# A four-layer graph transformer on one core: other chunk sizes at the end of a layer, the last V in one piece, V earlier in layer 3

## The chip, the cores and the metric

The kernel runs on one NeuronCore of a Trainium2 chip. The metric is the device time of one execution in microseconds; the number for the kernel before is the median of three runs. A profile is one further execution, recorded by the hardware profiler.

## The reference, cut to what matters

There are 3327 nodes with 256 features and a random adjacency matrix with about 0.5 per cent of ones, some 16 neighbours a node. Layer 0 is a small graph attention. Layers 1 to 3 are transformer layers in which a node attends to its neighbours only:

```python
qkv = layer_norm(x, g1, be1) @ w_qkv                 # 256 -> 768
q, k, v = ...                                        # 8 heads of 32
scores = jnp.einsum('nhd,mhd->hnm', q, k) * SCALE
scores = jnp.where(mask, scores, -jnp.inf)           # mask = adj != 0
attn = jax.nn.softmax(scores, axis=-1)
out = jnp.einsum('hnm,mhd->nhd', attn, v).reshape(n, DIM)
x = x + out @ w_proj + b_proj
h2 = layer_norm(x, g2, be2)
ff = jax.nn.gelu(h2 @ w1 + b1) @ w2 + b2             # 256 -> 1024 -> 256
return x + ff
```

Layer L+1 needs k and v of all nodes: a neighbour can lie anywhere.

## The kernel before, in words

**Phase 0** (lines 623 to 1208) reads the adjacency matrix, computes layer 0 and q, k, v of layer 1, lists every node's neighbours and sorts the nodes by their number of neighbours. After that there are 26 blocks of 128 nodes. Block b has `CAPS[b]` neighbour slots for each node, 40 for block 0 down to 10 for block 25.

**Layers 1 to 3** (class `Layer`, from line 1277) work on a table `kv[L]` in device memory, one row with k and v per node. `issue` (line 1288) fetches one *group*: up to four neighbour slots of one block, one indirect DMA (line 1303, on the GpSimd queue, POOL) for each slot, 128 rows of 2 KB each. The groups land in a ring of `NBUF` = 10 tiles. The blocks are taken in the order 25, 1, 24, 2, ..., 14, 12, 13, 0 (`ORDER`), so that block 0 with its ten groups comes last.

**A turn** of the loop in `run` (line 1568) handles one group:

- `scores` multiplies k by q (line 1325) and sums by head (line 1326), both on VectorE (DVE);
- after a block's last group `softmax` takes the minimum of the negated scores (line 1337, DVE) and the exponential (line 1340, ScalarE, ACT), and `take_q` copies the next block's q (line 1311, ACT);
- `value` does V for an earlier group: `weights` once for a block (lines 1346 to 1353, DVE), then `values`: v times weight (line 1366, DVE), then transposes that add the slots up in PSUM (line 1372, TensorE, PE). After that the tile of the ring is free, and `values` calls `issue` for the next group. V for a block begins in the second turn after its exponential. In the turns of block 0 two groups of V are done per turn;
- `some` (line 1544) hands out the rest of the work. There are two lists. `short` holds a finished block's copy (line 1390), projection (lines 1394 to 1396) and residual add with the statistics of the norm (line 1400). `long` holds the steps of a *chunk* of blocks, each with a cost.

**Chunks.** When the last block of a chunk has had its add, `chunk` (line 1411) puts these steps into `long`: the norm's scale (13 small DVE operations), the normalised blocks and their transposes (lines 588 and 591), up, Gelu and down in 8 pieces (lines 1439, 1445, 1462; line 1455 for a chunk of one block), shift and transposes back (lines 1468 and 1476), one add a block (line 1480), and in layers 1 and 2 the next layer's norm, q, k, v (`qkv`, line 1492) and `keep`, which copies k and v out of PSUM (line 1498), scales q (line 1499) and stores the row block to `kv[L + 1]` (line 1500). In layer 3 `store` writes the output instead (line 1505). The next layer's first gather waits until all rows are stored.

**The rate.** `self.rate` is credit per turn: the cost of all steps in `long`, divided by a number of turns (lines 1404 to 1407). It is set when a chunk's steps are added. Every call of `some` adds the rate to the credit, at most 8, and takes steps as long as the credit is above 0. Chunks before the change have 3, 4, 4, 4, 4, 4, 2 and 1 blocks. The divisor is the number of groups in the next four blocks less 2, and 5 for the chunk ahead of block 0. After the turns come the values that are left (block 0's ten groups), each followed by `some`; then `some` alone at rate 4.

The program order on each engine is the order in which these functions are called. Nothing is reordered later; an engine waits where its next instruction has to wait.

Of the kernel before, what the change touches and what calls it, by code (L numbers as in the profile page):

```python
# [8 lines left out]
FP = mybir.dt.float32  # L9
BF = mybir.dt.bfloat16  # L10
I32 = mybir.dt.int32
AF = mybir.ActivationFunctionType
# [5 lines left out]
P = 128  # L18
N = 3327
D = 256  # L20
HEADS = 8
# [11 lines left out]
NB = (N + P - 1) // P  # L33
# [27 lines left out]
CB = 4  # L61
# [447 lines left out]
@with_exitstack  # L509
def kernel(ctx: ExitStack, tc: tile.TileContext, ins, out: bass.AP):  # L510
    nc = tc.nc
    keep = ctx.enter_context(tc.tile_pool(name="s_keep", bufs=1))
    dram = ctx.enter_context(tc.tile_pool(name="s_dram", bufs=1, space=DRAM))
    flag = keep.tile([1, 1], I32, name="flag")
    E = mybir.EngineType
    with tc.manual_schedule(engines={E.PE, E.DVE, E.Activation, E.Pool, E.SP}):
        with ExitStack() as inner:
            sparse_path(inner, tc, ins, out, dram, flag)
    unfit = nc.values_load(flag[0:1, 0:1])
    with tc.If(unfit > 0):  # L520
        general_path(tc, ins, out)


def sparse_path(ctx, tc, ins, out, dram, flag):
    nc = tc.nc
    const = ctx.enter_context(tc.tile_pool(name="s_const", bufs=1))
    small = ctx.enter_context(tc.tile_pool(name="s_small", bufs=4))

    ident = const.tile([P, P], FP, name="s_ident")
# [12 lines left out]
    kv = {1: dram.tile([PADDED + 1, KVW[1]], FP, name="kv1"),  # L542
          2: dram.tile([PADDED, KVW[2]], FP, name="kv2"),
          3: dram.tile([PADDED, KVW[3]], FP, name="kv3")}
# [78 lines left out]
    with tc.tile_pool(name="a", bufs=1) as a, tc.tile_pool(name="aw", bufs=2) as aw, \  # L623
# [462 lines left out]
        for g in reversed(range(NG)):  # L1086
            at = dict(zip(names, (0, 1, 3, 4, 5, 6, 7, 8, 9, 10, 11, 12)))
# [179 lines left out]

    ORDER = [b for k in range(NB // 2) for b in (NB - 1 - k, k + 1)][:NB - 1] + [0]
    CHUNK, at = {}, 0
    for n in [CB - 1] + [CB] * ((NB - CB - 2) // CB) + [2, 1]:  # L1270
        for b in ORDER[at:at + n]:
            CHUNK[b] = ORDER[at:at + n]
        at += n
    assert at == NB
    slots = {b: [(b, s) for s in range(0, CAPS[b], GS)] for b in ORDER}

    class Layer:
# [102 lines left out]
        def block(self, b):  # L1380
            L, w, c = self.L, self.w, {}
            x = t2[:, b, :D]
            chunk = CHUNK[b]
            if b == chunk[0]:
                self.n2 = Norm(len(chunk), f"f{L}_{b}")
            n2 = self.n2

            def copy_T():
                c["oT"] = work.tile([P, 2 * P], FP, tag="oT", name=f"oT_{L}_{b}")
                nc.scalar.copy(c["oT"], self.po[b][:, :2 * P])  # L1390

            def project():
                ps = self.po[b][:, D:]
                nc.tensor.matmul(ps, ones_bf[:96, :], bias3[:, 0, :], start=True, stop=False)  # L1394
                for k in range(2):
                    nc.tensor.matmul(ps, c["oT"][:, k * P:(k + 1) * P], w["w_proj"][:, k, :],  # L1396
                                     start=False, stop=(k == 1))

            def add():
                nc.vector.tensor_add(x, x, self.po.pop(b)[:, D:])  # L1400
                n2.stats(chunk.index(b), x)
                if b == chunk[-1]:
                    self.long += self.chunk(chunk, n2)
                    at = ORDER.index(b) + 1
                    turns = sum(len(slots[i]) for i in ORDER[at:at + CB])
                    turns = 5 if at == NB - 1 else turns - 2
                    self.rate = sum(cost for cost, _ in self.long) / max(turns, 1)

            return [lambda: None, copy_T, project, lambda: None, add]

        def chunk(self, blocks, n2):
            L, w, nxt = self.L, self.w, self.nxt
            n = len(blocks) * P
# [81 lines left out]
            def keep(j):  # L1495
                b = blocks[j]
                kvr = work.tile([P, 2 * D], FP, tag="kvr", name=f"kvr_{L}_{b}")
                nc.scalar.copy(kvr, c["pk", j])
                nc.scalar.mul(t2[:, b, D:2 * D], c["pq", j][:, :D], -HD ** -0.5)
                nc.scalar.dma_start(kv[L + 1][b * P:(b + 1) * P, :], kvr)  # L1500

            def store(j):
                b = blocks[j]
# [27 lines left out]
            if nxt is not None:  # L1531
                steps += [at(2, lambda: c["n1"].scale()), *(at(2, t) for t in turns("n1", "n")),
                          at(2, lambda: to_hT("n1", "n", nxt["g1"], nxt["be1"])),
                          at(3, lambda: qkv(0))]
                for j in js:
                    fs = [lambda j=j: keep(j)]
                    if j + 1 < len(blocks):
                        fs.append(lambda j=j: qkv(j + 1))
                    steps.append(at(3, *fs))
            else:  # L1540
                steps += [at(1, lambda j=j: store(j)) for j in js]
# [12 lines left out]
                self.short.pop(0)()  # L1554

        def run(self):
            for _ in range(NBUF):
                self.issue()
            self.take_q(ORDER[0])

            todo, wait = [], {}

            def value():
                if todo[0][1] == 0:
                    self.weights(todo[0][0])
                self.values(*todo.pop(0))

            for k, b in enumerate(ORDER):
                for g in slots[b]:
                    self.scores(*g)  # L1570
                    if g == slots[b][-1]:
                        self.softmax(b)
                        if k + 1 < NB:
                            self.take_q(ORDER[k + 1])
                    for i in wait:
                        wait[i] += 1
                    for _ in range(2 if len(todo) > NBUF // 2 or b == 0 else 1):
                        if todo and wait[todo[0][0]] > 1:
                            value()
                    self.some()  # L1580
                todo += slots[b]
                wait[b] = 0
            while todo:
                value()
                self.some()
            self.rate = 4.0
            while self.short or self.long:
                self.some()
# [45 lines left out]
```

## Time and profile before

| what | us |
|---|---|
| median of three runs | 2573.75 (2568.12 to 2575.34) |
| the profiled execution | 3158.07 |
| its span, first to last instruction | 3156.3 |
| POOL: first gather of layer 2 | 1428.53 |
| POOL: last gather of layer 1 begins | 1310.82 |
| busy: DVE, PE, POOL, ACT | 1935.3, 1794.0, 1362.7, 774.6 |
| gathers of k and v rows (line 1303) | 1344, of 947 ns each |
| scores: multiply, sum (lines 1325, 1326) | 363 each, of 1138 and 1141 ns |
| V multiply (line 1366) | 363, of 1128 and 1221 ns |
| mean granted PE clock | 0.735 |

The profiled execution took 584 us longer than the median of the runs. So shares of the span are not shares of the metric, and a stage's length is taken over only where the text says why. "Busy" counts the time an instruction executes. The forty slices of the page are 78.9 us each, a digit is a tenth of busy time. "A <- B: total, times, longest" in the list of waits means that the engine and line A stood still until B ended; "remote" is a wait whose releaser the profile can't name, "issue" time without a wait that it shows.

### The profile page before, as it was taken

Reading aid. Unit: us, or ns where it says so; the run is one execution under the profiler, and the core shown is the slowest. Engines: PE = TensorE matmul, PEld = TensorE weight load, DVE = VectorE, ACT = ScalarE, POOL = GpSimd, SP = SyncE. Lnnn points to the kernel's source line nnn. Section 1 sums busy time; section 2 is a strip of 40 time slices with the busy share of each in tenths; the row PEclk is TensorE's granted clock in tenths of the full one; section 3 lists DMA queues with packets and bytes.
Section 4 is the critical chain, followed back from the end, with each engine's and each line's share of the span. In section 5 each row is a group of like instructions: output and inputs, shape, how many; then the busy total and the mean of one; then the engine's idle time right before and its main releaser. Section 6 shows DMA issues by size and latency. Waiting matters only on the chain.

```text
span 3156.3 us, 24036 instructions
## 1 busy us (share of the span) xinstructions
PE 1794.0 (57%) x7561; PEld 1163.5 (37%) x7561; DVE 1935.3 (61%) x3983; ACT 774.6 (25%) x1316; POOL 1362.7 (43%) x1458
## 2 busy tenths in 40 slices
PE   4767752255666666671457667666713435665556
PEld 3645531133333333350334333433512323433334
DVE  6688995457657656533656756755446556656554
ACT  4455621012222222230112212222300111212112
POOL 4000004545555554305555555544054555565550
PEclk9868766577787886785578778878755766776768
DMA  5334306645555565415455555555064554554560
GB/s 207 131 117 148 129 31 204 174 138 169 165 172 162 156 174 152 112 51 177 141 156 156 163 160 150 175 152 140 24 189 125 156 155 135 169 163 147 161 156 13
DMA packets 144486, 453.80 MB, mean 144 GB/s; under 512 B 29521, under 2 KB 40156, under 8 KB 141021
## 3 DMA queue, kind: packets, MB, share of 16 engines
q0 software_dynamic: 113056, 370.26, 40.9%
q1 hardware_dynamic: 9834, 53.90, 4.9%
q10 hardware_dynamic: 21458, 28.02, 2.5%
q8 instruction: 61, 1.00, 0.1%
q14 instruction: 77, 0.63, 0.1%
HBM read 420.64 MB, written 31.42 MB: 143 GB/s over the span
## 4 chain that ended last, share of the span: by engine, by line
DVE 25%; issue 18%; PE 18%; another core or an unknown queue 17%; POOL 11%; ACT 5%; DMA 5%; DVEq 0%; ACTq 0%; POOLq 0%; SPq 0%
POOL kv L1303 11%; DVE kv L1325 5%; DMA kv<-kv,t 4%; DVE sc L1326 3%; DVE vw L1366 3%; PE pu L1439 3%; PE po L1372 3%; PE py L1462 2%; DVE cand L735 2%; PE pk L1492 1%; PE s_pk L1010 1%; ACT s_aT L724 1%; DVE s_v L731 1%; PE pf L591 1%
## 5 line engine op out<-in xcount | busy, mean ns | idle before, releaser
L1303 POOL DMA_INDIRECT kv<-kv,t x1344 | 1273.0, 947 | 1210.3 <-issue 534.2
L1372 PE MATMUL po<-s_ident,vw 128*128 128x128 f32 x2688 | 475.4, 334 | 580.2 <-DVE vw L1366 387.2
L1372 PEld LDWEIGHTS po<-s_ident,vw 128*128 128x128 f32 x2688 | 395.5, 174 | 724.1 <-issue 373.5
L1325 DVE TENSOR_TENSOR kv<-kv,q 128x1024 f32<-128x1024 f32 (+3 forms) x363 | 413.1, 1138 | 397.1 <-ACT q L1311 274.6
L1366 DVE TENSOR_TENSOR vw<-kv,w 128x1024 f32<-128x1024 f32 x333 | 371.4, 1128 | 87.2 <-remote 84.6
L1326 DVE TENSOR_REDUCE sc<-kv 128x32 f32<-128x1024 f32 (+3 forms) x363 | 414.1, 1141 | 12.4
L1439 PE MATMUL pu<-fT,s_w 128*128 128x512 f32 (+3 forms) x768 | 341.2, 579 | 62.3 <-issue 35.8
L1462 PE MATMUL py<-gT,s_w 128*128 128x512 f32 (+2 forms) x672 | 321.8, 597 | 58.1 <-issue 50.2
L1400 DVE TENSOR_TENSOR t<-t,po 128x256 f32<-128x256 f32 x78 | 32.6, 418 | 390.8 <-remote 254.5
L1445 ACT ACTIVATE gT<-pu,pvb 128x512 f32<-128x512 f32 (+3 forms) x192 | 115.7, 607 | 628.2 <-remote 384.1
L1439 PEld LDWEIGHTS pu<-fT,s_w 128*128 128x128 f32 x768 | 157.4, 222 | 196.1 <-issue 146.4
L1462 PEld LDWEIGHTS py<-gT,s_w 128*128 128x128 f32 x672 | 132.6, 206 | 180.7 <-issue 144.0
L1396 PEld LDWEIGHTS po<-s_w_proj,oT 128*128 128x128 f32 x312 | 71.8, 255 | 281.8 <-issue 272.3
L1394 PE MATMUL po<-bias,s_ones_bf 96*128 96x256 bf16 x78 | 25.2, 324 | 259.7 <-issue 147.4
L1390 ACT COPY oT<-po 128x256 f32<-128x256 f32 x78 | 28.9, 371 | 548.5 <-remote 320.2
L711 POOL MEMSET s_abf<- 128x1 bf16 x23 | 2.2, 104 | 361.4 <-DVE s_v L731 253.7
L1492 PE MATMUL pk<-s_w_qkv,nT 128*128 128x512 f32 x208 | 128.4, 748 | 22.0 <-ACT nT L596 9.9
L735 DVE MAX8 cand<-s_v 128x8 f32<-128x208 bf16 x416 | 118.0, 360 | 0.9
L1396 PE MATMUL po<-s_w_proj,oT 128*128 128x256 f32 x312 | 113.1, 500 | 0.0
L723 PE MATMUL s_ptb<-s_ident_bf,s_abf 128*128 128x128 bf16 x676 | 67.1, 265 | 68.3 <-ACT s_abf L714 45.2
L591 PE MATMUL pf<-s_ident,xn_f 128*128 128x128 f32 x156 | 46.1, 444 | 86.8 <-ACT xn_f L588 66.7
L855 PE MATMUL s_pa<-s_aT,s_hs 128*128 128x256 bf16 x338 | 82.3, 290 | 13.2 <-DVE s_hs L817 13.2
(288 smaller groups left out, 2252.1 us busy)
## 6 DMA issues: line engine op xcount, KB each, us to landing
s_a<-in_adj_dram SPq DMA_DIRECT2D x25, 1663.5 KB
kv<-kv,t POOLq DMA_INDIRECT x1344
kv<-kvr ACTq DMA_DIRECT2D x52, 256.0 KB
kv<-s_kvr ACTq DMA_DIRECT2D x26, 256.0 KB
s_w<-in_L_gnn_w_dram SPq DMA_DIRECT2D x6, 1024.0 KB
t<-ql ACTq DMA_DIRECT2D x6, 592.0 KB
t<-s_x ACTq DMA_DIRECT2D x6, 512.0 KB
s_w_qkv<-in_L_gnn_w_qkv_dram SPq DMA_DIRECT2D x3, 768.0 KB
```

Source lines behind the costliest of these rows:

```text
L735: nc.vector.max(out=self.cand[:, s, :], in_=self.v[:, s, :])
L855: nc.tensor.matmul(self.pa[:, c0:c0 + 2 * P], S.hs[:r, k, :P], aT[:r, k, :], start=(k == 0), stop=(k == NB - 1))
L1303: nc.gpsimd.indirect_dma_start(out=t[:, s, :], out_offset=None, in_=kv[L], in_offset=bass.IndirectOffsetOnAxis(ap=t2[:, b, k:k + 1].bitcas ...
L1325: nc.vector.tensor_mul(k, k, self.q[b][:, None, :].to_broadcast([P, n, D]))
L1326: nc.vector.tensor_reduce(self.sc[b][:, s0:s0 + n, :], k.rearrange("p s (h d) -> p s h d", d=HD), AX.X, ALU.add)
L1366: nc.vector.tensor_mul(vw[:, :n * D].rearrange("p (s h d) -> p s h d", h=HEADS, d=HD), v, self.wp[b][:, s0:s0 + n, :, None].to_broadcast([ ...
L1372: nc.tensor.matmul(self.po[b][:, k * P:(k + 1) * P], vw[:, at:at + P], ident, is_transpose=True, start=(s0 + s == 0 and k == 0), stop=(s0 ...
L1396: nc.tensor.matmul(ps, c["oT"][:, k * P:(k + 1) * P], w["w_proj"][:, k, :], start=False, stop=(k == 1))
L1439: nc.tensor.matmul(c["pu", f][:, :n], w["w1"][:, e, f * P:(f + 1) * P], c["hT"][:, e, :n], start=(e == 0), stop=(e == 1))
L1445: nc.scalar.activation(g[:, :n], c.pop(("pu", f))[:, :n], AF.Gelu_apprx_tanh, bias=w["b1"][:, f:f + 1])
L1462: nc.tensor.matmul(c["py"][e][:, :n], w["w2"][:, f, e * P:(e + 1) * P], g[:, :n], start=(f == 0), stop=last)
L1492: nc.tensor.matmul(ps[:, :c1 - c0], c["hT"][:, e, j * P:(j + 1) * P], nxt["w_qkv"][:, e, c0:c1], start=(e == 0), stop=(e == 1))
```

## The change

- The chunks become 3, 4, 4, 4, 4, 3, 3, 1: the last three are 10, 15, 11; then 14, 12, 13; then 0. They were 10, 15, 11, 14; 12, 13; and 0.
- The divisor of the rate counts the groups of the next chunk, less 2, less 1 where the next chunk is smaller, less 4 for the chunk ahead of block 0.
- The values left after the last turn are done without `some` between them.
- In layer 3, where there is no next layer, V begins one turn after the exponential instead of two.
- Ahead of those last values ACT executes one Gelu of 8 columns whose result nothing reads.
- `keep` stores the rows of k and v ahead of scaling q.

```diff
-    for n in [CB - 1] + [CB] * ((NB - CB - 2) // CB) + [2, 1]:
+    for n in [CB - 1] + [CB] * ((NB - 10) // CB) + [3, 3, 1]:
...
-                    turns = sum(len(slots[i]) for i in ORDER[at:at + CB])
-                    turns = 5 if at == NB - 1 else turns - 2
+                    ahead = CHUNK[ORDER[at]] if at < NB else []
+                    turns = sum(len(slots[i]) for i in ahead)
+                    turns -= 4 if at == NB - 1 else 1 if len(chunk) > len(ahead) else 2
                     self.rate = sum(cost for cost, _ in self.long) / max(turns, 1)
...
                 nc.scalar.copy(kvr, c["pk", j])
+                nc.scalar.dma_start(kv[L + 1][b * P:(b + 1) * P, :], kvr)
                 nc.scalar.mul(t2[:, b, D:2 * D], c["pq", j][:, :D], -HD ** -0.5)
-                nc.scalar.dma_start(kv[L + 1][b * P:(b + 1) * P, :], kvr)
...
+            behind = 2 if self.nxt else 1
...
-                        if todo and wait[todo[0][0]] > 1:
+                        if todo and wait[todo[0][0]] >= behind:
                             value()
...
+            table = small.tile([P, HEADS], FP, tag="table", name=f"table_{L}")
+            nc.scalar.activation(table, ident[:, :HEADS], AF.Gelu_apprx_tanh)
             while todo:
                 value()
-                self.some()
```

More of the change, by code (lines that the diff above doesn't have):

```diff
@@ L1556, in run @@
         def run(self):
+            L = self.L
             for _ in range(NBUF):
```

## The prediction

> **What bounds the kernel now.** I read first the page's busy shares and its forty slices, then the waits, then the stages at the ends of the layers, then those stages instruction by instruction.
>
> ```profile
> PE 1794.0 (57%) x7561; PEld 1163.5 (37%) x7561; DVE 1935.3 (61%) x3983; ACT 774.6 (25%) x1316; POOL 1362.7 (43%) x1458
> ...
> POOL 4000004545555554305555555544054555565550
> ```
>
> No engine is full. POOL is the one that falls to 0, at two layer ends and at the end of the kernel. There no gather is issued.
>
> ```profile
> ACT gT L1445 <- remote: 384.1, 31, 29.6
> ...
> POOL kv L1303 <- DVE vw L1366: 372.7, 66, 16.5
> ...
> POOL kv L1303 <- DVE s_part L1255: 116.8, 1, 116.8
> ...
> POOL kv L1303 <- DVE s_row L1259: 114.1, 1, 114.1
> ```
>
> The two single waits of 116.8 and 114.1 us are the ends of layers 1 and 2: POOL waits until the last rows of the next layer are stored. With the last end, 3069 to 3156.3 (87.3), that is 318 us. The "remote" waits lie inside the gather stretches; nothing in the trace names what ACT waits for.
>
> The profiled execution took 3158.07 us (span 3156.3, 1.8 around it), the median of three runs is 2573.75. Which stage holds the difference? The page shows one gather every 1.25 us where POOL runs freely (0.947 busy, 0.30 between). If phase 0 (about 495) and the ends (318) cost the same in both, 2573.75 - 495 - 318 = 1761 us remain for 1370 gathers of rows, 1.28 us each. So I read the timed runs as close to POOL's own pace between the ends, and the profiled one as stretched there. A gain in the middle is then worth little, and one at a layer end counts in full. I add my changes in microseconds to the median.
>
> Now the end of layer 1, one engine after the other (start, length).
>
> ```profile
> 1318.72 0.42 DVE L1400 TENSOR_TENSOR t<-t,po 128x256 f32<-128x256 f32 x1 [17.80 <-PE po L1396]
> ...
> 1356.35 0.73 DVE L1346 TENSOR_REDUCE den<-sc 128x8 f32<-128x320 f32 x1 [9.94 <-ACT sc L1340]
> ...
> 1378.07 0.42 DVE L1480 TENSOR_TENSOR t<-t,pd 128x256 f32<-128x256 f32 x1 [16.69 <-PE pd L1476]
> ...
> 1399.22 0.42 DVE L1400 TENSOR_TENSOR t<-t,po 128x256 f32<-128x256 f32 x1 [2.85 <-PE po L1396]
> ```
>
> ```profile
> 1340.13 3.78 PE L1492 MATMUL pk<-s_w_qkv,nT 128*128 128x512 f32 x4 [0.66 <-ACT nT L596]
> 1343.70 1.91 PE L1492 MATMUL pq<-s_w_qkv,nT 128*128 128x256 f32 x4
> ...
> 1358.49 3.78 PE L1439 MATMUL pu<-fT,s_w 128*128 128x256 f32 x8 [0.44 <-ACT fT L596]
> ```
>
> ```profile
> 1422.04 0.58 ACT L1498 COPY kvr<-pk 128x512 f32<-128x512 f32 x1 [2.95 <-PE pk L1492]
> 1422.90 0.38 ACT L1499 ACTIVATE t<-pq 128x256 f32<-128x256 f32 x1 [0.28 <-PE pq L1492]
> 1422.91 0.39 ACTq L1500 DMA_DIRECT2D kv<-kvr  x1
> ```
>
> I count from block 13's residual add, 1318.72. Then three chunks pass one after another: the rest of the four-block chunk until its last q at 1354, the two-block chunk 1356 to 1392 with block 0's V pieces between (DVE waits 16.69 us), block 0 alone from its add at 1399.22 to its row store at 1422.91. The first gather follows at 1428.53: **109.8 us** in all.
>
> **What the Trainium skill says.** "TensorE: Matmul & The Clock Gate", section "What's actually happening": after idling the PE runs at half rate, and about 3.4 us of work release it. The trace agrees: the first 8 records of 256 columns take 3.78 us where later ones take 1.72. I add 2 us wherever PE restarts. "ScalarE: Activation LUTs", section "What ACT_TABLE_LOAD costs": about 1283 ns; the trace has 1283 for both kinds. "DMA: Bandwidth & Descriptors", section "Issuing engines are not separate DMA queues": stores and weight reads share the same engines. The 5.6 us from row store to first gather, with weights being read, fit; only the store's start moves here.
>
> **The change part by part.**
>
> *Chunks.* Turns of block 0 are numbered 1 to 10 (four gathers each). By the costs in the code, the four-block chunk before spreads over turns to block 0's turn 9, the two-block one starts in turn 10. After: blocks 10, 15, 11 end in turn 4, and 14, 12, 13 start in turn 6, after block 13's add in turn 5 as before. Rate 61.0/6 = 10.2 brings them up to their second norm's scale by turn 10; their turning, q, k and v come after V. Chain for layers 1 and 2 after that add (t = 0), rows of the trace:
> - add and statistics 1.1, one score group 2.4, scale 2.6 (13 small DVE operations): 6.1. Normalise and turn three blocks 4: 10.
> - Feed-forward of 384 columns: 16 steps of 1.29 us (0.86 at 256 columns) = 20.6, cold start 2: 33. DVE finishes its four scores meanwhile (2.4 each; the last gather, about 20 us after t by POOL's order, is no limit).
> - ACT: two shifts 1.1, then exp with its load 1.28 + 0.56: 36. DVE: three adds with statistics 3.2, scale 2.6: 41, softmax weights 1.6: 42.6.
> - *Last V in one go*: 10 x 1.13 = 11.5, its PE transposes (1.0 each) beside it and 1.1 after: 55.2. Here V stands in the open; before, about half lay beside the two-block chunk. The removed calls only hand out steps later.
> - PE is in order, so the chunk's turning waits for V: 57.3; projection of block 0 to 58.6; q, k, v of three blocks 3 x 2.58: 67.0; ACT's last copies 67.4. Block 0's add and scale (3.6) lie beside it.
> - Block 0: its normalise and turn 2, feed-forward 9, add, scale, turn 6, k and v 3.2, copy 0.6: 88. To the first gather 5.6: **93.5**.
>
> 109.8 - 93.5 = **16.3 us** per layer, twice: 32.6. Layer 2 before has the same length (116.2 of POOL silence against 116.7).
>
> *Rows ahead of q.* The store is queued behind a multiply that waits for the q matmuls: issued 1422.91, possible at 1422.62. 0.3 us at a layer end (in the 93.5), for 52 blocks. Behind it on ACT stands the multiply and what follows, later by one issue (0.33), where ACT idles. Bounds: 0.3 gained, 0.33 lost; nothing else moves past it, POOL's and SP's queues stay as they are.
>
> *Early Gelu load.* One extra small operation and the same load, 1.28 us, placed while V runs on DVE. Before, layer 3 loads exp and Gelu in the middle of the two-block chunk, PE losing 0.6. Worth 0 to 0.6; without V as cover, 1.5 lost. I take 0.
>
> *V one group behind exp in layer 3.* W waits for exp, but the next block's scores already wait for q, which ACT copies after exp; so no new DVE wait. Nothing in POOL's pace improves. It releases ring tiles one turn earlier.
>
> *Layer 3's end* has no q, k, v. Before: 3075.87 (block 13's add) to 3128.30 (block 0's), 52.4. After: same start to 10; Gelu of the three-block chunk done after 14 steps: 30.5; exp 32.4; weights 34; V 45.5; three adds, then projection 48.3 (store and block 0 follow as now). **4.1 us**.
>
> *Ahead of t.* After block 13's last V, PE has before four feed-forward steps (6.9 us) ahead of its projection, after one block's q, k, v (2.6); in layer 3 5.2 against 0. Bound 0 to 13.8 for three layers; the scores of turn 5 wait for a gather, so half: 6.
>
> *Compressed rates.* The chunk 8, 17, 9, 16 gets 13 turns for 16, rate 5.65 for 4.59: in its feed-forward PE has 2.8 x 1.72 = 4.9 plus V's 1.0 to 1.7 in a turn of 5.0 us (four gathers): over-full by about 1 us for six turns. Its shift, back and first adds now fall in one turn, so DVE waits there, and behind DVE's add stand the V that free ring tiles. Not in the trace: between 0 (the ring covers it) and 8 us per layer; 3 each in layers 1 and 2, as the excess is 6 and half has cover. In layer 3 the rate is 4.2 and I take 0. Sum 6.
>
> Sum: 32.6 + 4.1 + 6 - 6 = 36.7. **2573.75 - 37 = 2537 us**; 3158 would become about 3121, if its stretched parts stay.
>
> **The rivals.**
> *Slower: PE's over-full turns starve the ring.* If the wait for the compressed chunk's adds outlasts the gathers in flight, POOL idles, and at its pace every idle microsecond is kernel time. For: PE busy reaches 25 of 30 us in some windows; POOL waits 372.7 us for V. Against: that excess is only 6 us per chunk. It decides above 36.7 / 2 = 18 us in each of layers 1 and 2 (without the gain ahead of t); at 24, 2573.75 - 36.7 + 48 = 2585.
> *The end only changes its wait.* V alone and the wider last chunk stand in the open. If the six turns are emptied later than I count (gathers or an ACT wait like the remote ones of 20 us), the end saves 4 instead of 16 us per layer: 2573.75 - 12 = 2562.
> *More than summed.* The whole 13.8 ahead of t, no rate cost, and ring tiles freed earlier worth 10 in layer 3: 2573.75 - 36.7 - 13.8 - 10 = 2513.
> That the change doesn't do what it says is only possible for the Gelu load, worth under 2 us.
>
> **How the numbers follow.** Forecast 0.62, unchanged end 0.17, more 0.11, slower 0.10. A measurement of this kernel tells about 0.3% (7.7 us) from no change. Half of the unchanged-end case lies within that: faster 0.62 + 0.11 + 0.09 = 0.82, same 0.08, slower 0.10. Range: the bounds give 2523 to 2553 for the forecast; with most of the two milder rivals 2515 to 2565.
>
> **What would show it.** In the trace after: from block 13's add to the next layer's first gather about 93 us (layers 1 and 2), ten V in a row on DVE in 11.5 us, POOL silent for about 98 instead of 116; from that add to block 0's in layer 3 about 48. The windows of chunk 8, 17, 9, 16 show DVE waiting for "pd" little more than now. Wrong if that wait grows past 8 us per layer, if POOL's waits for V grow, or if q, k, v of the last three-block chunk run past t + 67.

## The result, and the profile after

| | median, us | lowest to highest | ratio to before, 95% interval |
|---|---|---|---|
| before, 5 runs | 2570.82 | 2565.11 to 2575.34 | 1 |
| after, 5 runs | 2555.91 | 2555.05 to 2560.22 | 0.9947 [0.9933, 0.996] |

The change saves 15 us, 0.5 per cent; the forecast was 37. Because the first profile of before took 3158 us and the kernel before took 3120 to 3146 us beside runs f1, f2, f3, h1 and i1, for a reason that no trace shows, all comparisons below are with a second profile of before (e0_before: 2565.71 us, span 2563.9), and those five runs are read only as ratios.

In the profile of after, the busy times and the forty slices of POOL:

```profile
PE 1667.7 (65%) x7561; PEld 1119.4 (44%) x7561; DVE 1939.2 (76%) x3983; ACT 781.8 (31%) x1321; POOL 1361.1 (53%) x1458
...
POOL 4000000177777776631777767656137767777671
```

The work is what it was; POOL still falls to 1 at each layer end. In the waits of after (engine and line, what it waited for, total, times, longest), and then of before, the two layer ends and POOL's waits for V:

```profile
POOL kv L1303 <- DVE s_row L1259: 78.9, 1, 78.9
POOL kv L1303 <- DMA colsa<-in_L_gnn_be_dram: 75.7, 1, 75.7
...
POOL kv L1303 <- DVE vw L1366: 56.3, 35, 12.5
```

```profile
POOL kv L1303 <- DVE s_row L1259: 97.5, 1, 97.5
...
POOL kv L1303 <- DVE s_part L1255: 96.8, 1, 96.8
...
POOL kv L1303 <- DVE vw L1366: 39.4, 38, 3.1
```

Each end is some 20 us shorter for POOL, which alone would be 40 us. But its waits for V have grown, the longest from 3.1 to 12.5 us.

Block 13's residual add is the moment t, as in the prediction. Here it is in layer 1 of before (start, length; in brackets the idle time before and what ended it):

```profile
1094.86 0.42 DVE L1400 TENSOR_TENSOR t<-t,po 128x256 f32<-128x256 f32 x1 [4.76 <-PE po L1396]
```

The end of layer 1 in the trace of after, VectorE:

```profile
1109.22 0.42 DVE L1400 TENSOR_TENSOR t<-t,po 128x256 f32<-128x256 f32 x1 [2.19 <-PE po L1396]
...
1143.98 0.42 DVE L1481 TENSOR_TENSOR t<-t,pd 128x256 f32<-128x256 f32 x1 [8.58 <-PE pd L1477]
...
1151.08 4.63 DVE L1366 TENSOR_TENSOR vw<-kv,sc 128x1024 f32<-128x1024 f32 x4
1155.87 6.90 DVE L1366 TENSOR_TENSOR vw<-kv,sc 128x1024 f32<-128x1024 f32 x6
1166.41 0.42 DVE L1400 TENSOR_TENSOR t<-t,po 128x256 f32<-128x256 f32 x1 [3.64 <-PE po L1396]
```

and ScalarE, with the load that the change puts there, the last row store ahead of its multiply:

```profile
1145.25 1.28 ACT L1589 ACT_TABLE_LOAD   x1
...
1193.65 0.33 ACTq L1500 DMA_DIRECT2D kv<-kvr  x1
1194.03 0.38 ACT L1501 ACTIVATE t<-pq 128x256 f32<-128x256 f32 x1 [0.40 <-PE pq L1493]
```

Here t is 1109.22, the ten V stand in one row of 11.7 us, block 0's add follows at t + 57.2, its row store at t + 84.4, layer 2's first gather at 1196.67, t + 87.5. The prediction had 11.5, 58.6 (for the projection), 88 and 93.5. So the end went as drawn, up to 6 us faster. But t itself came later. That is seen when each layer is cut at t:

| us, from the profiles | before | after | difference |
|---|---|---|---|
| layer 1: first gather to t | 591.3 | 604.8 | +13.5 |
| layer 1: t to layer 2's first gather | 105.9 | 87.5 | -18.4 |
| layer 2: first gather to t | 579.9 | 595.0 | +15.1 |
| layer 2: t to layer 3's first gather | 106.2 | 90.2 | -16.0 |
| layer 3: first gather to t | 594.9 | 594.7 | -0.2 |
| layer 3: t to the end | 82.1 | 76.6 | -5.5 |
| three layers | 2060.3 | 2048.9 | -11.4 |

The ends give 39.9 us, and 28.4 of them are paid back ahead of t. (Phase 0, which the change doesn't touch, differs by a few us from profile to profile, so the sum over the layers is the better number below.)

**Where t is lost.** Count from the second group of block 11, turn 95 of a layer's 121. Up to it the two kernels take the same time from the layer's first gather, to 1.2 us in layer 1 and 0.1 in layer 2. Views over stretches of time of layer 1: before (first line to t, second from t to the next layer), then the same of after; columns: stretch, length, then busy time with instructions of PE, PE's loads, DVE, ACT, POOL, then PE clock, DMA share, GB/s.

```profile
984.80:1094.90 110.10, 89.64 (x355) 54.42 (x354) 92.11 (x153) 35.61 (x78) 80.05 (x85) 0.88 0.76 215
1094.90:1200.80 105.90, 70.42 (x299) 49.61 (x297) 45.97 (x122) 30.57 (x63) 6.99 (x9) 0.84 0.30 74
```

```profile
984.40:1109.20 124.80, 95.89 (x399) 62.10 (x397) 96.76 (x174) 39.30 (x89) 77.92 (x83) 0.88 0.66 190
1109.20:1196.70 87.50, 61.57 (x253) 40.63 (x253) 41.26 (x100) 26.46 (x53) 9.07 (x11) 0.84 0.37 85
```

The stretch ahead of t grew by 14.7 us. 6.3 us of that is PE work (95.89 - 89.64) that used to be done behind t: the end has 8.9 less. The other 8.4 is PE standing idle. On DVE, the busiest engine of the stretch, 4.7 us is more work (96.76 - 92.11), and its waits of over 0.9 us sum to 24.5 us after against 15.0 before. Those of over 4 us in after:

```profile
1008.66 0.42 DVE L1481 TENSOR_TENSOR t<-t,pd 128x256 f32<-128x256 f32 x1 [8.33 <-PE pd L1477]
...
1061.05 1.22 DVE L1325 TENSOR_TENSOR kv<-kv,q 128x1024 f32<-128x1024 f32 x1 [5.68 <-ACT q L1311]
...
1081.25 0.42 DVE L1481 TENSOR_TENSOR t<-t,pd 128x256 f32<-128x256 f32 x1 [4.67 <-PE pd L1477]
```

The first is chunk 8, 17, 9, 16, the other two are chunk 10, 15, 11. Before has no wait of over 2.6 us in this stretch up to block 0's first scores, one of 4.64 for q at them and the 4.76 at t. Layer 2 of after shows the same three: 8.33, 6.00, 4.67. From that second group of block 11 to the third of block 12 DVE takes 57.6 us after and 49.5 before; from there to block 0's first group 45.0 and 35.6. What PE does in the first of these waits (PE in the trace of after):

```profile
996.80 1.88 PE L1463 MATMUL py<-gT,s_w 128*128 128x512 f32 x4
998.52 1.04 PE L1372 MATMUL po<-s_ident,vw 128*128 128x128 f32 x8
999.39 1.88 PE L1440 MATMUL pu<-fT,s_w 128*128 128x512 f32 x4
1001.11 1.88 PE L1463 MATMUL py<-gT,s_w 128*128 128x512 f32 x4
1002.83 1.04 PE L1372 MATMUL po<-s_ident,vw 128*128 128x128 f32 x8
1003.70 3.60 PE L1463 MATMUL py<-gT,s_w 128*128 128x512 f32 x8
1007.14 0.82 PE L1372 MATMUL po<-s_ident,vw 128*128 128x128 f32 x6
1007.79 1.27 PE L1477 MATMUL pd<-s_ident,yT 128*128 128x128 f32 x8
```

No row has a bracket: PE is full without a gap and runs behind DVE, which had its last V multiply done at 1000.3. The chunk's first add stands in DVE's order ahead of the next scores, so DVE waits out PE's whole lag. In before PE is nearly as full (gaps of 0.45 and 0.14 us from 980 to 1012), but the work is spread over more turns: the last down ends only 2.1 us later, and the first add stands behind two more groups, where the transposes are done and no wait shows (PE and DVE in the trace of e0_before):

```profile
1005.82 3.60 PE L1462 MATMUL py<-gT,s_w 128*128 128x512 f32 x8
...
1011.52 0.39 DVE L1480 TENSOR_TENSOR t<-t,pd 128x256 f32<-128x256 f32 x1
```

POOL doesn't ride over this. A tile of the ring is free only after its V, and V stands behind the add in DVE's order. In layer 2 of after, where the same wait of 8.33 us ends at 1691.16, the trace names V as what POOL waited for:

```profile
1705.22 0.94 POOL L1303 DMA_INDIRECT kv<-kv,t  x1 [12.46 <-DVE vw L1366]
```

Two more such waits, 4.65 and 7.80 us, follow before t. In before POOL's longest wait in this stretch of layer 2 is 3.10 us.

And the 5.68 us on DVE: ScalarE copies the next block's q behind the exponential, and this stands behind Gelus that wait for PE (ScalarE in the trace of after):

```profile
1057.08 0.58 ACT L1446 ACTIVATE gT<-pu,pvb 128x384 f32<-128x384 f32 x1 [2.56 <-PE pu L1440]
1058.37 0.58 ACT L1446 ACTIVATE gT<-pu,pvb 128x384 f32<-128x384 f32 x1 [0.71 <-PE pu L1440]
1058.85 0.18 ACT L1329 CAST t<-kv 128x1 int32<-128x1 f32 x1
1059.05 1.28 ACT L1340 ACT_TABLE_LOAD   x1
1060.34 0.41 ACT L1340 ACTIVATE sc<-sc,mx 128x136 f32<-128x136 f32 x1
1060.66 0.36 ACT L1311 COPY q<-t 128x256 f32<-128x256 f32 x1
```

### The profile page after: what moved, and what is told of

The parts are those of the page before. It is cut to its first block, busy times and chain, and to the rows that moved or that the text cites. A ratio compares the mean times of both kernels' runs of the same rounds, so it can differ in the third digit from the quotient of the medians.

```text
span 2553.3 us, 24048 instructions
## 1 busy us (share of the span) xinstructions
PE 1667.7 (65%) x7561; PEld 1119.4 (44%) x7561; DVE 1939.2 (76%) x3983; ACT 781.8 (31%) x1321; POOL 1361.1 (53%) x1458
## 4 chain that ended last, share of the span: by engine, by line
PE 17%; DVE 15%; DMA 12%; POOL 9%; issue 9%; ACT 2%; DVEq 0%; ACTq 0%; POOLq 0%; SPq 0%
DMA kv<-kv,t 11%; POOL kv L1303 8%; PE pu L1440 5%; PE py L1463 4%; DVE kv L1325 4%; PE po L1372 3%; DVE vw L1366 3%; DVE sc L1326 3%; PE pk L1493 2%; PE po L1396 1%; POOL out_dram L1506 1%; DVE t L1481 1%; DVE st_n L575 1%; PE py L1456 0%; PE pq L1493 0%
## 5 line engine op out<-in xcount | busy, mean ns | idle before, releaser
L1372 PE MATMUL po<-s_ident,vw 128*128 128x128 f32 x2688 | 456.3, 327 | 514.0 <-DVE vw L1366 512.8
L1372 PEld LDWEIGHTS po<-s_ident,vw 128*128 128x128 f32 x2688 | 381.4, 170 | 641.5 <-DVE vw L1366 543.7
L1440 PE MATMUL pu<-fT,s_w 128*128 128x512 f32 (+2 forms) x768 | 322.8, 555 | 2.9 <-ACT fT L596 2.9
L1463 PE MATMUL py<-gT,s_w 128*128 128x512 f32 (+1 forms) x672 | 283.6, 550 | 0.0
L1446 ACT ACTIVATE gT<-pu,pvb 128x512 f32<-128x512 f32 (+2 forms) x192 | 116.6, 608 | 380.0 <-PE pu L1440 379.5
L1440 PEld LDWEIGHTS pu<-fT,s_w 128*128 128x128 f32 x768 | 151.8, 211 | 124.8 <-issue 91.1
L1493 PE MATMUL pk<-s_w_qkv,nT 128*128 128x512 f32 x208 | 109.6, 653 | 6.1 <-ACT nT L596 6.1
L588 ACT ACTIVATE xn_f<-t,nm_f,rqy_f 128x256 f32<-128x256 f32 x78 | 43.2, 594 | 217.7 <-DVE nm_f L582 211.0
L591 PE MATMUL pf<-s_ident,xn_f 128*128 128x128 f32 x156 | 46.0, 436 | 97.7 <-ACT xn_f L588 97.5
L1340 ACT ACTIVATE sc<-sc,mx 128x120 f32<-128x120 f32 (+6 forms) x78 | 32.0, 410 | 204.9 <-DVE mx L1337 204.4
L723 PEld LDWEIGHTS <-s_abf 128*128 128x128 bf16 x676 | 56.6, 122 | 78.3 <-ACT s_abf L714 55.0
L724 ACT COPY s_aT<-s_ptb 128x896 bf16<-128x896 bf16 x104 | 82.3, 859 | 20.5 <-PE s_ptb L723 20.5
```

Of the source, the lines that this page charges most:

```text
L723: nc.tensor.transpose(pt[:, m, :], self.abf[:, k * P:(k + 1) * P], ident_bf)
L1372: nc.tensor.matmul(self.po[b][:, k * P:(k + 1) * P], vw[:, at:at + P], ident, is_transpose=True, start=(s0 + s == 0 and k == 0), stop=(s0 ...
L1440: nc.tensor.matmul(c["pu", f][:, :n], w["w1"][:, e, f * P:(f + 1) * P], c["hT"][:, e, :n], start=(e == 0), stop=(e == 1))
L1446: nc.scalar.activation(g[:, :n], c.pop(("pu", f))[:, :n], AF.Gelu_apprx_tanh, bias=w["b1"][:, f:f + 1])
L1463: nc.tensor.matmul(c["py"][e][:, :n], w["w2"][:, f, e * P:(e + 1) * P], g[:, :n], start=(f == 0), stop=last)
L1493: nc.tensor.matmul(ps[:, :c1 - c0], c["hT"][:, e, j * P:(j + 1) * P], nxt["w_qkv"][:, e, c0:c1], start=(e == 0), stop=(e == 1))
```

## The experiments

Ratios are to the kernel before, timed beside each run (medians 2569.59 for e0 to e3, 2567.59 for e4 to e7, 2570.94 for g, 2567.95 for j). "Layers" is the sum over the three layers in the profile: 2060.3 before, 2048.9 after. The two stage numbers are layer 1 / layer 2.

| run | us | ratio, interval | first gather to t | t to next layer | layers |
|---|---|---|---|---|---|
| e1 chunks and rates alone | 2572.72 | 1.0014 [1.0005, 1.0022] | 606.1 / 595.8 | 97.2 / 97.3 | 2066.9 |
| e2 last V in one go alone | 2562.78 | 0.9976 [0.9965, 0.9987] | 591.2 / 580.5 | 105.3 / 105.8 | 2057.0 |
| e3 V earlier in layer 3 alone | 2569.5 | 0.9999 [0.9991, 1.0007] | 591.3 / 583.5 | 105.7 / 106.2 | 2063.7 |
| e4 after, work between last V | 2570.9 | 1.0011 [1.0003, 1.0019] | 606.0 / 597.1 | 92.4 / 96.8 | 2063.2 |
| e5 after, V in layer 3 as before | 2557.84 | 0.996 [0.9947, 0.9972] | 606.0 / 598.5 | 87.4 / 90.2 | 2052.4 |
| e6 after, old rates | 2563.19 | 0.9977 [0.997, 0.9984] | 585.0 / 573.6 | 108.9 / 108.5 | 2055.6 |
| e7 after, old chunks and rates | 2561.92 | 0.9973 [0.9962, 0.9984] | 591.4 / 579.8 | 102.6 / 105.4 | 2053.7 |
| g1 after, chunk 8, 17, 9, 16 over 16 turns | 2546.67 | 0.9909 [0.9895, 0.9923] | 599.5 / 593.3 | 87.2 / 89.9 | 2038.9 |
| g2 g1, and 10, 15, 11 over 14 turns | 2548.66 | 0.9913 [0.99, 0.9927] | 593.0 / 581.6 | 97.4 / 98.0 | 2038.5 |
| g3 after, four-block chunk's adds later | 2575.24 | 1.0018 [1.0007, 1.0029] | 615.4 / 604.0 | 88.8 / 91.1 | 2070.7 |
| j1 after, 10, 15, 11 alone over 14 turns | 2565.93 | 0.9993 [0.9982, 1.0003] | 606.0 / 598.0 | 94.7 / 92.8 | 2062.0 |
| j2 after once more | 2556.38 | 0.9964 [0.9949, 0.9979] | 605.2 / 595.1 | 87.5 / 90.1 | 2048.2 |

### The parts alone

e0_before is the kernel before, profiled a second time.

> The kernel before once more, to get an execution that isn't stretched in its gather stretches (its first profile took 3158 us). Theory A (the ends gain what was forecast, the middle gives it back): POOL is silent about 97 us between layers 1 and 2 and again between 2 and 3, against 79.0 and 75.7 in the changed kernel, and from block 13's add to the next first gather it is about 107; then the gather stretches must be shorter than those of the changed kernel by some 20 to 25 us in all. Theory B (the ends were never as long as the stretched profile showed): POOL is silent about 82 to 85 us, and the gather stretches have the same length in both.

It took 2565.71 us; its stages are the column "before" above. POOL is silent for 96.8 and 97.5 us, and the three stretches up to t are 28.4 us shorter in all than after: this is theory A.

e1 makes the chunks and rates of the change and leaves the rest:

```diff
-    for n in [CB - 1] + [CB] * ((NB - CB - 2) // CB) + [2, 1]:
+    for n in [CB - 1] + [CB] * ((NB - 10) // CB) + [3, 3, 1]:
...
+                    turns -= 4 if at == NB - 1 else 1 if len(chunk) > len(ahead) else 2
```

> Chunk sizes and rates alone; block 0's V still with other work between, V two turns behind exp everywhere. Theory A: the ends gain, the compressed rates cost in the middle: 2555 to 2565. Theory B: the gain of 15 us is nearly all here: 2553 to 2558. A third view, that V in one go is what costs: below 2550.

Measured 2572.72, outside all three forecasts: by themselves the chunks gain nothing. Their t is 14.9 and 15.9 us later and their ends 8.7 and 8.9 shorter. So the loss ahead of t belongs to this part and to no other.

e2 takes only the `some` between the last values away:

```diff
             while todo:
                 value()
-                self.some()
```

> Block 0's V in one go alone, with the chunks of before. The two-block chunk then begins in turn 10 of block 0 and its up, down, q, k, v all stand after V instead of beside it. Both theories: slower than before by about half of V's 11.5 us at each of three ends less the DVE waits that go, 0 to 15 us: 2571 to 2586.

Measured 2562.78: that was a miss, it gains 6 to 7 us by itself in the timed runs. Below are DVE's V pieces of layer 1's end, in the traces of e0_before and of e2:

```profile
1131.15 3.49 DVE L1366 TENSOR_TENSOR vw<-kv,sc 128x1024 f32<-128x1024 f32 x3
...
1150.57 0.42 DVE L1480 TENSOR_TENSOR t<-t,pd 128x256 f32<-128x256 f32 x1 [15.92 <-PE pd L1476]
...
1155.15 3.49 DVE L1366 TENSOR_TENSOR vw<-kv,sc 128x1024 f32<-128x1024 f32 x3
1158.85 1.23 DVE L1366 TENSOR_TENSOR vw<-kv,sc 128x1024 f32<-128x1024 f32 x1 [0.21 <-PE po L1372]
1165.27 3.50 DVE L1366 TENSOR_TENSOR vw<-kv,sc 128x1024 f32<-128x1024 f32 x3 [5.19 <-PE po L1372]
1171.61 0.42 DVE L1400 TENSOR_TENSOR t<-t,po 128x256 f32<-128x256 f32 x1 [2.85 <-PE po L1396]
```

```profile
1131.43 3.50 DVE L1366 TENSOR_TENSOR vw<-kv,sc 128x1024 f32<-128x1024 f32 x3
1136.50 8.04 DVE L1366 TENSOR_TENSOR vw<-kv,sc 128x1024 f32<-128x1024 f32 x7 [1.57 <-PE po L1372]
1150.22 0.42 DVE L1400 TENSOR_TENSOR t<-t,po 128x256 f32<-128x256 f32 x1 [5.69 <-PE po L1396]
```

With other steps between, ten pieces take 37.6 us (1131.15 to 1168.77), in one go 13.1. The 15.92 us is DVE standing at the two-block chunk's first add, which it must do ahead of the remaining V; the 5.19 us is DVE waiting for V's own transposes, which stand in PE's order behind steps of the chunk. Block 0's add comes 21.4 us earlier; but the two-block chunk, pushed back, then ends nearly as late as before (105.3 us from t to the next layer against 105.9), so most of it isn't kept here. The three ends of e2's profile are only 1.1 us shorter in all than those of e0_before. Where the rest of the 6 to 7 us lies the traces don't show; e0_before's own time is 4 us under the median of before.

e3 has only V one group behind in layer 3:

```diff
-                        if todo and wait[todo[0][0]] > 1:
+                        if todo and wait[todo[0][0]] > (1 if self.nxt else 0):
```

> V one group behind exp in layer 3 alone. Theory A as forecast: nothing in the middle, the end of layer 3 earlier by 0 to 5 us: 2566 to 2571. If POOL waited for ring tiles in the timed runs: 2555 to 2563. If V then waits for exp on DVE: 2573 or more.

Measured 0.9999: no effect that can be told.

### One part undone

e4 gives the `some` between the last values back, in the kernel after:

```diff
             while todo:
                 value()
+                self.some()
```

> The changed kernel, but with other work handed out again between block 0's last ten V. Theory C (chunk work moved ahead of block 13's add comes back as a later add; V in one go is then a gain of its own, since between the V pieces PE's program order holds V behind steps that wait for ACT): from that add to the next first gather 97 us instead of 87.5 and 90.3, 2555.9 + 9.7 + 7 = 2571 to 2574. Forecast's own view (V in one go exposes V, other work beside it is cover): the same or faster, 2545 to 2556.

Measured 2570.9, as theory C had it to 0.1 us: all of the gain is gone. The ends are 4.9 and 6.6 us longer (theory C had 97 in both layers), and t is 1 to 2 later. The chunks pay only together with V in one go.

e5 has V two groups behind in all layers (`behind = 2`).

> The changed kernel with V two groups behind exp in layer 3 too. Forecast and theory C: layer 3 changes by 0 to 4 us, 2554 to 2560. If the early V pays in layer 3 because the three-block chunk ends earlier there: 2560 to 2565.

Measured 0.996 against 0.9947 for the change, and the intervals overlap: with e3, no effect that can be told.

e6 keeps the new chunk sizes and takes the old formula of the rates: 16 turns for 8, 17, 9, 16 (13 in the change), 21 for 10, 15, 11 (11), and 5 for 14, 12, 13 (6).

> The changed kernel with the rates of before: the chunk 10, 15, 11 gets 21 turns instead of 11, so its second half falls behind block 13's add again. Theory C: that add comes back by about 14 us in layers 1 and 2 (some 580 us after the layer's first gather in layer 2 instead of 595), and the way from it to the next first gather grows from 87.5 to 110 to 120, because the three-block chunk then lies behind V: 2580 to 2600. If the sizes and not the rates held block 13's add back: it stays late and the total passes 2600.

The total I expected was missed by far; what came out was 2563.19. The direction is right: t is 20 us earlier than in the change and the end 21 and 18 longer. Between these two, work moves across t nearly one for one.

e7 takes the old sizes and rates:

> The changed kernel with the chunk sizes and rates of before: V in one go, V one group behind in layer 3, rows ahead of q, early Gelu load. If the parts add up, V in one go (2562.8 alone) with the others worth nothing: 2560 to 2564. If the new chunks are what makes V in one go pay (theory C): not below 2560. If the chunks only cost: 2550 to 2555.

It gives 2561.92, the same as e2: early table load, rows ahead of q and layer 3's V add nothing that can be told. So of the 15 us some 6 to 7 come from V in one go alone, the rest from it and the chunks together.

### The loss ahead of t

g1 takes one of the two places away: the chunk 8, 17, 9, 16 gets its 16 turns back. Theory D, in what follows, says that t is late for two separate costs of about 9 us each in layers 1 and 2, one from this chunk and one from 10, 15, 11. Theory C says that work is only moved about.

```diff
-                    turns -= 4 if at == NB - 1 else 1 if len(chunk) > len(ahead) else 2
+                    turns -= 4 if at == NB - 1 else -2 if len(chunk) > len(ahead) else 2
```

> As f1_c4_16, which fell on a chip where the kernel before takes 3120 us. Theory D: 2538 to 2543, block 13's add 7 to 9 us earlier than in the changed kernel in layers 1 and 2, the end 87 to 91. Theory C: 2552 to 2558.

Measured 2546.67, between the two forecasts. It beats both kernels, and its interval lies apart from that of the change (0.9933 to 0.996): 24.3 us below before, 9 to 10 below the change (medians, layers). The 8.33 us wait is gone, and with it the waits of 5.68 and 4.67, up to block 0's first group: the two stretches of 57.6 and 45.0 us take 49.6 and 37.0, near to before. But the adds of chunk 10, 15, 11 now stand behind that group, and other waits show in the trace of g1:

```profile
1073.82 1.22 DVE L1325 TENSOR_TENSOR kv<-kv,q 128x1024 f32<-128x1024 f32 x1 [7.41 <-ACT q L1311]
...
1079.27 0.42 DVE L1481 TENSOR_TENSOR t<-t,pd 128x256 f32<-128x256 f32 x1 [1.51 <-PE pd L1477]
...
1105.46 0.42 DVE L1400 TENSOR_TENSOR t<-t,po 128x256 f32<-128x256 f32 x1 [4.12 <-PE po L1396]
```

The first is block 0's first group, waiting for the q that is copied behind chunk 10, 15, 11's Gelus; from it to block 0's third group g1 takes 16.9 us, the change 9.5. So t is only 5.3 and 1.7 us earlier than in the change, at the same length of the end.

g2 stretches that chunk too, `-2` as in g1 and `-1 if at == NB - 4`:

> As f2_c4_16_c5_14, on such a chip too (0.988 of the kernel before there, against 0.999 of f1). Theory D: 2540 to 2548. Theory C: 2550 to 2558. By the order on the other chip it is the faster of the two, so 2535 to 2545 if that order holds.

Measured 2548.66. Now t is within 2 us of where before has it (593.0 / 581.6), but the end is 97.4 and 98.0. In the stretch view of g2, to t and from t:

```profile
989.50:1101.40 111.90, 89.39 (x376) 58.24 (x375) 97.52 (x175) 36.47 (x81) 82.28 (x88) 0.87 0.76 216
1101.40:1198.80 97.40, 72.60 (x279) 45.40 (x277) 40.82 (x100) 29.27 (x61) 4.76 (x6) 0.83 0.28 72
```

PE's 6 us of work are back behind t, and the end is 10 us longer for it. So this second place is no loss that can be taken away: it is work that must stand on one side of t or the other.

j1 asks the same with the first place left as in the change:

```diff
+                    turns -= 4 if at == NB - 1 else 1 if len(chunk) > len(ahead) else -1 if at == NB - 4 else 2
```

> The change with the work of chunk 10, 15, 11 alone spread over 14 turns (11 in the change), once more. Where the kernel before takes about 2570 us: two separate costs give 2553 to 2559 with block 13's add 6 to 10 us earlier, one and the same work moved about gives 2566 to 2574. Where the kernel before takes about 3130 us: within 0.3 per cent of the change beside it.

Measured 2565.93, which is what "moved about" gives, 10 us worse than the change beside it: t isn't earlier (606.0 / 598.0) and the ends are 7.2 and 2.6 longer. Counted from turn 95, block 0's first group comes 8 us earlier, its third no more than 0.4: the lag of the first place is then met in block 0's turns. So the two places are not two separate costs that add up.

g3 tried to take the wait without touching the rate, with the transposes back held until the credit allows, at a cost of 5 in place of 1.5 in four-block chunks.

> As f3_add_later. If DVE's 8.3 us in one turn are the cause: 2540 to 2548. If it only waits for the same PE backlog a turn later: 2553 to 2558.

A miss: 2575.24. The higher cost also raises the rate of each four-block chunk, as the rate is the sum of costs over the turns, and t is 10.6 and 8.9 later still, so the total says nothing about the wait itself. The trace of g3 does: the 8.33 us at the add is gone, and the next thing in DVE's order that hangs on PE, block 14's q behind ScalarE's work for that chunk, waits in its place:

```profile
1022.56 1.22 DVE L1325 TENSOR_TENSOR kv<-kv,q 128x1024 f32<-128x1024 f32 x1 [9.71 <-ACT q L1311]
```

So it is PE's backlog that DVE meets, wherever the add stands.

j2 is the change once more:

> The change itself beside it. Where the kernel before takes about 2570 us: 0.993 to 0.997 of it, as in the first result. Where the kernel before takes about 3130 us the gathers run slower than POOL's pace, the layer ends cost as much as elsewhere, and DVE and PE have more time between gathers, so that block 13's add is hardly later and more of the end's gain is left: 15 to 40 us less than before, 0.987 to 0.995.

0.9964, a saving of 12 us, with stages within 0.6 us of the first profile of after.

f1, f2, f3 are the kernels of g1, g2, g3, h1 and i1 that of j1. Their ratios to the kernel before beside them are 0.9986 [0.9966, 1.0006], 0.9876 [0.9841, 0.9911], 1.0028 [1.0009, 1.0046], 1.001 [0.9991, 1.0028], 0.9974 [0.9954, 0.9994]. Their order differs (f2 gains most), and the change itself has no run beside them, so I draw nothing from them.

## Why the prediction was wrong

| step | forecast | measured |
|---|---|---|
| ends of layers 1 and 2 | -32.6 | -34.4 |
| end of layer 3 | -4.1 | -5.5 |
| ahead of t and compressed rates, three layers | -6 + 6 = 0 | +28.4 |
| sum | -36.7 | -11.4 (medians: -15) |

**The ends** were right in size and in mechanism: one chunk's feed-forward, V in a row, the q, k, v behind it, block 0 alone. In layer 3 block 0's add came 49.3 us behind t where 48 was forecast. In layers 1 and 2 the single points were a few us earlier than forecast, although the restart of PE cost 3.0 us and not 2 (the first 12 records of 384 columns took 7.06 us, 12 later ones 4.03). It is in part luck that the difference fits so well: the prediction's 109.8 came from the first profile, where layer 2's end was 107.2 with POOL silent for 114.1 us (not the same length, and not 116.2), and the second profile has 105.9 and 106.2.

**"Ahead of t" failed, by what it left out.** The step looked only at PE's queue right behind block 13's last V and took 6 us of gain. That gain came: DVE's wait for PE at t fell from 4.76, 4.75 and 3.48 us in the three layers to 2.19, 2.19 and none. But the step never added up all work that has to be done before t. Three blocks must be complete by then where before only a part of four was: 6.3 us of PE and 4.7 of DVE more in layer 1. g2 shows that it can be put back, and that the end then pays.

**"Compressed rates" had the right mechanism and a third of the size.** It took an excess of 6 us on PE, half covered: 3 per layer. DVE waits 8.33 us, in layers 1 and 2 alike. The ring doesn't cover it: the stretch with the wait is 8.1 us longer, and POOL stands still for 12.46 us behind it in layer 2. DVE has no slack there either: before, its work of 92 us and its waits of 15.0 fill 107 of 110 us. Undone alone (g1) it gave 9 to 10 us in all, not 16.7. The 11 turns of chunk 10, 15, 11 were not costed at all, though their rate of 61 over 11 and its Gelus ahead of q are as readable in the code as the other.

**The assumption under both was half right**: between the ends the kernel before does run near POOL's pace. In layer 1 464 gathers at 1.25 us make 580 of the 591.3 us up to t, in layer 2 441 make 551 of 579.9. What didn't follow is that a few us on DVE or PE then cost little: DVE was nearly as full, and its waits stop POOL. The first profile, with DVE at 61 per cent, hid this; in the second it is 76. For POOL's silence I had 116 falling to 98; it was 96.8 falling to 75.7. Only the difference carried over.

**The signs.** Of the three that would show the forecast wrong two came: the wait for "pd" grew to 8.33 us, past 8, and POOL's waits for V grew. The third didn't: the last q of the three-block chunk is done at t + 65.

**V in one go** was counted as a loss of cover that the chunks outweigh. The timed runs give it a gain by itself (e2, e7), of which the traces place little; without it the chunks gain nothing (e1, e4), and in the changed kernel it is worth 4.9 and 6.6 us at the ends of layers 1 and 2.

**V one group behind in layer 3, rows ahead of q, early table load**: 0, 0.3 and 0 forecast, nothing measurable (e3, e5, e7).

**The rivals.** The slower one named the mechanism that did occur: DVE held by the compressed chunk, and POOL idle for want of free tiles. Its point of decision was 18 us in each of layers 1 and 2; 13.5 and 15.1 came, for the two steps together, so it fell short of that point by little. The unchanged end, at 2562, was nearer to the measured time than the forecast for a reason that did not occur.

**What g1 leaves.** Its t is 5.3 and 1.7 us earlier than in the change, that of g2 11.8 and 13.4, that of e6 19.8 and 21.4. Counted from turn 95 g1's is 6.6 and 5.1 earlier; but its turn 95 is 1.3 and 3.4 us later, of which 1.1 and 3.3 are there at turn 85, where the two kernels don't yet differ. In layer 1 DVE's waits of over 0.9 us up to t then sum to 16.8 us (24.5 after, 15.0 before, 10.4 in g2), so most of the added waiting is gone, and what stays is mainly more work on DVE, 97.4 us against 92.1 before. g2 has as much of it; its t is earlier because 6 us of PE's work lies behind t and DVE has less to wait for. Open is whether some order of the steps avoids the 7.41 us for q without a longer end: no run here tried it.

## What to carry to other kernels

When a deadline is moved forward, count all work of every engine that now has to lie ahead of it, not only the queue in front of the marked instruction; what leaves the tail is paid before it unless an engine there idles. Steps that are spread by a rate need the rate checked against the busiest engine of that very stretch, and here it was best to slow the one chunk that overfilled it (g1). Before dropping steps between pieces of a dependent chain as "cover", look whether in-order queues make the pieces wait for these steps.

## What the runs showed of the hardware

A table load of 1.28 us on ScalarE costs by its place. At 1145.25 in the trace of after it lies beside DVE's work and nothing waits for it; at 1059.05 it lies between the late Gelus and the q that DVE waits 5.68 us for, 1.28 of them the load. In before the same load, at 1000.18, stands ahead of a q that DVE waits only 2.56 us for: so it is part of such a wait and not all of it. I had also not expected what taking steps out from between pieces of V does: 37.6 us fall to 13.1 for the same ten pieces.
